# Another order of issue for the first image of a four-layer vision kernel, and weighing before copying in layer 1

## The chip, the cores and the metric

The kernel runs on one core of a Trainium2 chip. Its engines each work through their own queue in order: TensorE (PE, matmuls; PEld is its weight load), VectorE (DVE), ScalarE (ACT), GpSimd (POOL) and SyncE (SP, which here only issues DMAs). ACT and POOL issue DMAs too. The metric is the device time of one execution in microseconds, lower is better. All data are float32; one float32 matmul appears in the trace as two PE instructions.

## The reference

The input is a batch of four images of 32 x 32 pixels with 384 channels. Four residual layers follow one another, each on a group-normalized input (32 groups of 12 channels):

```
x = x + L0(gn(x))   # deformable attention, 6 heads of 64
x = x + L1(gn(x))   # attention weighted by a group similarity, 12 heads of 32
x = x + L2(gn(x))   # box-filtered energy ratio
x = x + L3(gn(x))   # 3 x 3 outlook attention
```

Layer 0, cut to what matters:

```
q = x @ w_q + b_q
o = gelu(layernorm(grouped 3x3 conv(q)))                 # 6 groups of 64 channels
offset = tanh(o @ w_offp) * 16 ; pos = offset + pixel    # per group and pixel
xs = bilinear_sample(x, pos)                             # a gather of 1024 positions in 6 groups
k = xs @ w_k + b_k ; v = xs @ w_v + b_v
bias = bilinear_sample(rpe, (pixel - pos) / 2)           # 1024 x 1024 per head
out = softmax(q k^T / 8 + bias) v @ w_out + b_out
```

Layer 1, the part that the change touches, per head:

```
sim = sigmoid(beta + alpha * cos(xg, gc))                # 1024 x 256
gw  = (sim sim^T) * gamma + (1 - gamma)                  # 1024 x 1024, symmetric
a   = softmax(q k^T / sqrt(32)) * gw
a   = a / (sum of a over the queries + 1e-8) ; out = a v
```

## The kernel before

An image's channels lie in 3 blocks of 128 partitions (KC), its 1024 pixels in 8 tiles of 128 (NJ). Two lanes of work are issued by Python generators. The *front* (class Front) computes layer 0 of one image; the *trunk* (class Trunk) computes layers 1 to 3 of the image before it. `Net.layer0` (L266) issues the whole of layer 0 of image 0 alone; from then on `Net.layer3` (L280) steps the trunk of image b and, after each step, as many steps of the fronts of images 1 to 3 as keep them level. Within this program a planner of the framework chooses each engine's order: an instruction may be moved ahead of its place in the program if its inputs and memory are free in the planner's model; `keep_in_program_order` (the name `pin`) forbids that for single instructions. The framework also puts a wait between two engines that use the same PSUM bank, in program order, and between users of the same SBUF memory.

SBUF scopes are stacked from two sides: the front's on the right, the trunk's on the left; a scope's tiles can be written once the tiles that lay there before are released. PSUM holds two tiles of two banks (`big`) and four of one bank (`bank`). Weights rotate through three buffers (`weights`, L242).

Image 0, in the order of the program:

- `consts` (L107) loads small constants: `rows` (a row of 874 KB once broadcast to 128 partitions, L128), `hall` (L138), `Wa` (L154) on SP, others on ACT; it computes `gam` by a sigmoid on ACT (L158) and `half` on DVE (L166).
- `normed` (L551) loads the image on SP (L557), transposes it on PE (L567), copies it on ACT (L572) and normalizes it by `norm_steps` (L329), a generator that yields between the two sums over groups (PE, L345) and what reads them. For image 0 it calls `windows` (L173), which interpolates the table of `rpe` to half steps (DVE, L185 to L192; `half`, L193) and cuts it into 6 x 16 overlapping strips by six DMAs in DRAM, issued on ACT (L198). Then it transposes the normalized image, and ACT copies it (L596, two buffers) for SP to write to `pairs` in DRAM (L598).
- `inputs0` (L610) computes queries into `qpad` (L625), the grouped convolution (L644), the layer norm, the gelu and the positions (DVE), then gathers (POOL, L714) tile by tile, weighs on DVE (L727 to L730), transposes on PE (L741). After the last tile come the keys (`w_k`, L770, through DRAM `k0`) and then the values (`w_v`, L776, L777).
- `heads0` (L866) is a pipeline of 96 blocks (6 heads, 2 halves of queries, 8 tiles of keys), turn by turn, with DVE full almost throughout. From turn 17 on it takes one step of `early0` (L604) per turn, which normalizes image 1 ahead of time and stores it in DRAM (`xh1`). Each pair of heads ends in a division (`divide`, L913) of its block of `qpad`.
- `outputs0` (L457) multiplies `qpad` by `w_out` (18 matmuls by `dense_t`, L385: three blocks, two halves, three terms), adds the residual and stores `x1`.
- `Trunk.start` (L1115) loads `x1`, `image` (L1122) normalizes it; the front of image 1 begins with a load of `xh1` (L616, one DMA on SP) and its queries.

Layer 1 works on pairs of heads (`pair`, L1411). Each of its 6 pairs has 8 turns j; a turn computes two halves h of exponentials (`e`, L1486) and, for each half and each head r, one bank of group weights. Since these are symmetric, tiles above the diagonal are copied from the bank to `keep` by ACT (L1516; tiles `gn` and `gf`) and later transposed in place of a product (L1503). DVE weighs the exponentials by the bank and sums them (L1517). The next pair's row maxima and sums (`sums_step`, L1342: PE L1351, DVE L1359, ACT L1360) are interleaved.

## Time and profile before

| what | us |
|---|---|
| median of three executions (4630.12 to 4641.2) | 4640.76 |
| the profiled execution | 4625.18 |
| its span, first to last instruction | 4623.3 |
| PE busy | 4160.8 |
| DVE busy | 3134.6 |
| ACT busy | 2282.3 |
| POOL busy | 969.4 |
| mean granted clock of PE, share of full speed | 0.946 |

A busy time is the sum over an engine's instructions; what is missing to the span is idle. The views used below: the table of stretches gives busy time between two points of time; the timeline gives instructions in order, each with its start, its duration and, in brackets, how long its engine was idle before it and whose result ended that; the table of waits sums these by pairs (engine, tile and line waiting, then the engine, tile and line waited for; us in total, times, longest); the chain is followed backwards from the last instruction, at each step to what released it. A name with q (ACTq, SPq) is the engine's sequencer issuing a DMA. L with a number is a line of the program.

### The profile page before, as it was taken

The numbers are of one execution on the slowest core, as the hardware profiler recorded it, in microseconds if no ns is written. First come the engines' busy times: TensorE is split into PE (matmuls) and PEld (weight loads), VectorE is DVE, ScalarE is ACT, GpSimd is POOL, SyncE is SP. The second block draws the span as 40 slices with busy tenths as digits, with TensorE's granted clock in tenths as the row PEclk, the third lists the DMA queues.
The fourth block names the chain that finished last, engine by engine and source line by source line (L and its number), as shares of the span: only waits on it lengthen the run. The fifth ranks groups of instructions, "written<-read, shape, count | busy, mean of one in ns | idle before, by whom it ended". The sixth has DMA issues, their size and how long they took to land.

```text
span 4623.3 us, 47195 instructions
## 1 busy us (share of the span) xinstructions
PE 4160.8 (90%) x15896; PEld 1796.5 (39%) x15896; DVE 3134.6 (68%) x5909; ACT 2282.3 (49%) x3631; POOL 969.4 (21%) x994
## 2 busy tenths in 40 slices
PE   5499789999999898999999989899999999999998
PEld 2233334333334453333333444343333335343444
DVE  3599555878777627677878744768787874565644
ACT  2166333666565314565666432456665641555532
POOL 0654213212112104311212110522121211000000
PEclk8799899999999988999999989899999998999988
DMA  6445234212212244311212133432121213310011
GB/s 126 135 141 143 84 100 134 79 52 69 58 51 63 85 118 148 103 44 51 81 52 78 38 100 121 141 102 63 46 67 40 74 38 122 102 34 24 23 37 41
DMA packets 232819, 370.99 MB, mean 80 GB/s; under 512 B 117732, under 2 KB 165697, under 8 KB 232577
## 3 DMA queue, kind: packets, MB, share of 16 engines
q1 hardware_dynamic: 171560, 201.49, 14.7%
q0 software_dynamic: 39936, 145.53, 10.3%
q10 hardware_dynamic: 21080, 20.96, 1.8%
q8 instruction: 126, 2.06, 0.2%
q14 instruction: 117, 0.95, 0.1%
HBM read 287.90 MB, written 80.27 MB: 80 GB/s over the span
## 4 chain that ended last, share of the span: by engine, by line
PE 37%; DVE 8%; ACT 6%; issue 4%; DMA 2%; POOL 1%; SPq 0%; ACTq 0%; POOLq 0%; DVEq 0%
PE bank L1508 8%; PE big L1478 4%; PE bank L855 3%; PE bank L820 3%; PE big L1351 3%; PE bank L409 2%; ACT big L1360 2%; PE bank L1503 2%; PE big L395 2%; PE bank L1450 2%; DVE nmax L1359 2%; DVE e L1517 2%; PE bank L1188 1%; PE big L1633 1%; PE bank L1801 1%
## 5 line engine op out<-in xcount | busy, mean ns | idle before, releaser
L1508 PE MATMUL bank<-whole,sg 128*128 128x512 f32 (+3 forms) x2304 | 852.8, 505 | 8.3 <-POOL sg L1461 6.9
L1517 DVE SCALAR_TENSOR_TENSOR e<-bank,gam,e 128x512 f32<-128x512 f32 x768 | 561.4, 748 | 435.8 <-ACT gf L1516 157.5
L1360 ACT ACTIVATE big<-big,nmax 128x1024 f32<-128x1024 f32 x384 | 418.6, 1090 | 355.4 <-DVE nmax L1359 354.6
L1486 ACT ACTIVATE e<-big 128x1024 f32<-128x1024 f32 x384 | 379.8, 1019 | 415.2 <-PE big L1478 409.9
L1508 PEld LDWEIGHTS bank<-whole,sg 128*128 128x128 f32 x2304 | 402.7, 197 | 370.2 <-issue 281.0
L1359 DVE TENSOR_REDUCE nmax<-big 128x1 f32<-128x1024 f32 x384 | 454.1, 1217 | 51.9 <-PE big L1351 50.9
L799 POOL DMA_INDIRECT win<-strips,widx x288 | 307.9, 1069 | 680.4 <-DVE z L812 403.7
L1461 POOL TENSOR_SCALAR sg<-whole,gam 128x512 f32<-128x512 f32 x192 | 149.3, 780 | 1436.5 <-PE bank L1508 1013.3
L1478 PE MATMUL big<-qa,ka 64*128 64x512 f32 x1536 | 426.3, 627 | 11.2 <-ACT big L1360 10.7
L1351 PE MATMUL big<-k,q 32*128 32x512 f32 x1536 | 320.7, 659 | 78.8 <-ACT big L1360 40.0
L820 PE MATMUL bank<-qpad,kz 128*128 128x512 f32 x576 | 282.1, 618 | 12.4 <-DVE e L1517 12.4
L714 POOL DMA_INDIRECT gat<-pairs,sidx x192 | 207.3, 1079 | 386.3 <-DVE ix_gt L500 224.1
L855 PE MATMUL bank<-lg,va 128*64 128x512 f32 x576 | 263.7, 601 | 15.0 <-ACT lg L853 14.9
L855 PE MATMUL bank<-lg,ones 128*64 128x512 f32 x576 | 263.0, 601 | 0.0
L817 DVE SCALAR_TENSOR_TENSOR lg<-z,bias_f,lg 128x512 f32<-128x512 f32 x288 | 220.0, 772 | 37.8 <-ACT lg L816 36.4
L1478 PEld LDWEIGHTS big<-qa,ka 64*128 64x128 f32 x1536 | 138.8, 187 | 270.4 <-issue 157.1
L811 ACT ACTIVATE z<-win,bias_f 128x528 f32<-128x528 f32 x288 | 207.9, 738 | 58.5 <-DVE lg L817 26.3
L812 DVE SCALAR_TENSOR_TENSOR z<-win,bias_f,z 128x528 f32<-128x528 f32 x288 | 213.9, 759 | 25.5 <-ACT z L811 23.5
L852 DVE TENSOR_TENSOR lg<-lg,tb 128x512 f32<-128x512 f32 x288 | 187.5, 696 | 42.4 <-ACT tb L845 42.4
L1450 PE MATMUL bank<-e,vs 128*32 128x512 f32 x1536 | 206.7, 604 | 0.9 <-DVE vs L1444 0.9
L821 DVE TENSOR_TENSOR lg<-bank,lg 128x512 f32<-128x512 f32 x288 | 191.5, 683 | 21.3 <-PE bank L820 20.2
L816 ACT ACTIVATE lg<-z,bias_f 128x512 f32<-128x512 f32 x288 | 200.3, 718 | 11.3 <-DVE z L812 5.1
(313 smaller groups left out, 6617.7 us busy)
## 6 DMA issues: line engine op xcount, KB each, us to landing
pairs<-xn SPq DMA_DIRECT2D x64, 192.0 KB
q<-qd SPq DMA_DIRECT2D x48, 256.0 KB
w<-in_gmat SPq DMA_DIRECT2D x16, 576.0 KB
w<-in_w_off SPq DMA_DIRECT2D x12, 576.0 KB
w<-in_Wqkv SPq DMA_DIRECT2D x12, 576.0 KB
a<-in_x SPq DMA_DIRECT2D x16, 384.0 KB
x<-a ACTq DMA_DIRECT2D x4, 1536.0 KB
win<-strips,widx POOLq DMA_INDIRECT x384, 3.9
```

The lines of the kernel that those rows point to most:

```text
L799: nc.gpsimd.indirect_dma_start(out=win, out_offset=None, in_=self.strips[:, :], in_offset=bass.IndirectOffsetOnAxis(ap=self.widx[:, q, c : ...
L817: v.scalar_tensor_tensor(lg, z[:, :, 1 : HW + 1], sc(0, 0), lg, ALU.mult, ALU.add)
L820: nc.tensor.matmul(ps, kz[:, j * P : (j + 1) * P], both, start=True, stop=True)
L855: nc.tensor.matmul(po[out, :], w, lf, start=j == 0, stop=j == NJ - 1)
L1351: nc.tensor.matmul(ps[r][:, h * 512 : (h + 1) * 512], self.q4[rows, i * P : (i + 1) * P], self.k4[rows, 0:512], start=True, stop=True,)
L1359: v.tensor_reduce(nmax[:, r, i : i + 1], ps[r], AX.X, ALU.max, negate=True)
L1360: nc.scalar.activation(ps[r], ps[r], AF.Exp, bias=nmax[:, r, i : i + 1], accum_out=den[:, r, i : i + 1],)
L1450: nc.tensor.matmul(av[r0 : r0 + HD1, :], vs[:, r, :], es[h][:, r, :], start=j == 0, stop=j == NJ - 1,)
L1478: nc.tensor.matmul(ps[:, r, :], ka[rows, j * P : (j + 1) * P], qa[rows, cols], start=True, stop=True,)
L1486: nc.scalar.activation(e, ps, AF.Exp)
L1508: nc.tensor.matmul(ps[:, (mid - i0) * P :], sg[:, r, m, :], sim[:, h, r, m, (mid - i0) * P :], start=m == 0, stop=m == 1,)
L1517: v.scalar_tensor_tensor(e[:, r, :], ps, self.gam[:, 1:2], e[:, r, :], ALU.add, ALU.mult, accum_out=tot[:, r, h : h + 1],)
```

## The change

Image 0 and the start of image 1:

- `rows`, `hall` and `Wa` are loaded in a new function `more_consts`, called after the image's loads; `gam` and `half` are computed at the end of `windows`.
- The six strips are issued by a new function `cut`, on SP, after the convolution.
- `norm_steps` yields three times instead of once after each of its two sums. Only `early0` takes these yields one at a time.
- In the gather loop the values of tile j - 2 follow the weighing of tile j; `w_v` is loaded before the loop, the keys follow it, and the last tile's values come after the keys.
- `outputs0` of image 0 first issues the terms 0 and 1 of blocks 0 and 1, then the rest. It runs inside the heads' scope, its tiles on the left.
- Image 1's `xh1` is loaded by three DMAs on ACT.

For all images: in `pair`, ACT's copy to `keep` is issued after DVE's weighing of the same bank. No arithmetic changes.

```diff
@@ -124,8 +124,6 @@
                 )
-        self.rows = self.ct([P, NROW], "rows")
-        nc.sync.dma_start(self.rows, a["rows"].partition_broadcast(P))
         self.blk = self.ct([P, P], "blk")
@@ -134,8 +132,6 @@
         nc.gpsimd.memset(self.hall, 0.0)
-        for k in range(KC):
-            nc.sync.dma_start(self.hall[32 * k : 32 * k + 4, :], a["blk"][0::32, :])
         self.sel = self.ct([81, 9, 25], "sel")
@@ -150,23 +146,16 @@
+    def more_consts(self):
+        nc, a = self.nc, self.a
+        self.rows = self.ct([P, NROW], "rows")
+        nc.sync.dma_start(self.rows, a["rows"].partition_broadcast(P))
+        for k in range(KC):
+            nc.sync.dma_start(self.hall[32 * k : 32 * k + 4, :], a["blk"][0::32, :])
         self.wa = self.ct([P, KC, 81], "Wa")
...
-        self.gam = self.ct([P, 2], "gam")
-        nc.scalar.activation(
-            self.gam[:, 0:1], self.rows[:, R_SCAL + 2 : R_SCAL + 3], AF.Sigmoid
-        )
-        nc.vector.tensor_scalar(
-            self.gam[:, 1:2], self.gam[:, 0:1], -1.0, 1.0, ALU.mult, ALU.add
-        )
-        self.half = self.ct([P, 2], "half")
-        nc.vector.tensor_scalar(
-            self.half, self.rows[:, R_SCAL : R_SCAL + 2], 0.5, None, ALU.mult
-        )
     def col(self, i, k):
@@ -174,7 +163,7 @@
         v = nc.vector
-        half = self.dram.tile([G, UP, UP], F32, tag="half", name="half")
+        self.steps = half = self.dram.tile([G, UP, UP], F32, tag="half", name="half")
         self.strips = self.dram.tile([G * NSTRIP * STRIP, 1], F32, tag="strips", name="strips")
@@ -191,11 +180,28 @@
                 nc.scalar.dma_start(half[:, i::2, :].rearrange("g r c -> r g c"), u[0:m])
+        self.gam = self.ct([P, 2], "gam")
+        nc.scalar.activation(
+            self.gam[:, 0:1], self.rows[:, R_SCAL + 2 : R_SCAL + 3], AF.Sigmoid
+        )
+        nc.vector.tensor_scalar(
+            self.gam[:, 1:2], self.gam[:, 0:1], -1.0, 1.0, ALU.mult, ALU.add
+        )
+        self.half = self.ct([P, 2], "half")
+        nc.vector.tensor_scalar(
+            self.half, self.rows[:, R_SCAL : R_SCAL + 2], 0.5, None, ALU.mult
+        )
+    def cut(self):
         dst = self.strips.rearrange("(g s r c) o -> g s r (c o)", g=G, s=NSTRIP, c=WROW)
         for g in range(G):
-            row = half[g]
+            row = self.steps[g]
             src = bass.AP(row.tensor, row.offset, [[4, NSTRIP], [UP, UP], [1, WROW]])
-            nc.scalar.dma_start(dst[g], src)
+            self.nc.sync.dma_start(dst[g], src)
@@ -353,7 +359,7 @@
         sums = groups(mv[:, :, 0:1])
-        yield
+        yield from (None,) * 3
         nc.vector.tensor_scalar(mean, sums, 1.0 / 12.0, None, ALU.mult)
@@ -364,7 +370,7 @@
         sums = groups(d)
-        yield
+        yield from (None,) * 3
         nc.scalar.activation(rstd, sums, AF.Sqrt, bias=self.eps[:, 0:1], scale=1.0 / 12.0)
@@ -382,12 +388,14 @@
-    def dense_t(self, w, src, ko, lo=0):
+    def dense_t(self, w, src, ko, lo=0, kis=range(KC), ps=None):
         nc = self.nc
-        ps = self.big()
+        if ps is None:
+            ps = self.big()
         for h in range(2):
-            for ki in range(KC):
+            for ki in kis:
                 if len(src.shape) == 4:
@@ -439,7 +447,9 @@
                     yield from self.heads
-                yield from self.outputs0(b)
+                    self.side = "left"
+                    yield from self.outputs0(b)
+                    self.side = "right"
                 return
@@ -458,12 +468,21 @@
             w = self.weights("w_out")
+            ps = {}
+            if b == 0:
+                for ko in range(2):
+                    ps[ko] = self.dense_t(w, self.qpad, ko, kis=(0, 1))
             for ko in range(KC):
...
                 nc.sync.dma_start(x, self.x0[b % 2][rows, :])
-                ps = self.dense_t(w, self.qpad, ko)
-                v.scalar_tensor_tensor(x, ps, self.col(C_BOUT, ko), x, ALU.add, ALU.add)
+                if ko in ps:
+                    ps[KC] = self.dense_t(w, self.qpad, ko, kis=(2,), ps=ps[ko])
+                else:
+                    ps[KC] = self.dense_t(w, self.qpad, ko)
+                v.scalar_tensor_tensor(x, ps[KC], self.col(C_BOUT, ko), x, ALU.add, ALU.add)
                 nc.sync.dma_start(self.x1[b % 2][rows, :], x)
@@ -555,6 +574,8 @@
             nc.sync.dma_start(xin[:, j : j + 2, :], src[:, j : j + 2, :])
+        if b == 0:
+            self.net.more_consts()
         x = self.wt([P, KC, N], "a12", 2)
@@ -613,7 +634,8 @@
             xh = self.wt([P, KC, N], "a12", 2)
-            nc.sync.dma_start(xh, self.xh1.rearrange("(k p) n -> p k n", p=P))
+            for k in range(KC):
+                nc.scalar.dma_start(xh[:, k], self.xh1[k * P : (k + 1) * P, :])
             yield 25
@@ -653,6 +675,8 @@
             yield 15
+        if b == 0:
+            self.cut()
         oall = self.wt([P, NJ, C], "a12", 2)
@@ -750,6 +774,13 @@
         gats, xss = {0: gather(0), 1: gather(1)}, {}
+        va, bv = self.va, self.rows[:, R_BV0 : R_BV0 + C]
+        if b == 0:
+            w = self.weights("w_v")
+        def value(j):
+            v.tensor_tensor(va[:, j, :], self.dense_n(xsT, w, j), bv, ALU.add)
         yield 8
@@ -758,23 +789,23 @@
                 xss[j] = weigh(j, gats.pop(j))
+            if b == 0 and j > 1:
+                value(j - 2)
             if j > 0:
...
             next(self.heads)
-        va = self.va
         kT = self.wt([P, KC, N], "a12", 2)
-        w = self.weights("w_k")
+        wk = self.weights("w_k")
         for ko in range(KC):
-            ps = self.dense_t(w, xsT, ko)
+            ps = self.dense_t(wk, xsT, ko)
             v.tensor_scalar(kT[:, ko, :], ps, self.col(C_BK, ko), GC**-0.5, ALU.add, ALU.mult)
             nc.sync.dma_start(self.k0[ko * P : (ko + 1) * P, :], kT[:, ko, :])
-        bv = self.rows[:, R_BV0 : R_BV0 + C]
-        w = self.weights("w_v")
-        for j in range(NJ):
-            ps = self.dense_n(xsT, w, j)
-            v.tensor_tensor(va[:, j, :], ps, bv, ALU.add)
+        if b > 0:
+            w = self.weights("w_v")
+        for j in range(NJ - 1 if b == 0 else 0, NJ):
+            value(j)
         yield 30
@@ -1512,12 +1543,12 @@
                             )
-                    if first < i1:
-                        nc.scalar.copy(keep[:, r, :], ps[:, (first - i0) * P :])
                     v.scalar_tensor_tensor(
...
                     )
+                    if first < i1:
+                        nc.scalar.copy(keep[:, r, :], ps[:, (first - i0) * P :])
                 if h == 0 and st:
```

## The prediction

> **What bounds the kernel now.** I read the totals first, then busy time by stage, then the order of instructions inside the stages where TensorE is not full.
>
> ```profile
> PE 4160.8 (90%) x15896; PEld 1796.5 (39%) x15896; DVE 3134.6 (68%) x5909; ACT 2282.3 (49%) x3631; POOL 969.4 (21%) x994
> ```
>
> TensorE is the bound, and all it can win back is its 462 us of idle time. The next table gives, for each stretch, the busy time of PE, PE weight load, DVE, ACT and POOL, then the granted clock, the DMA share and GB/s.
>
> ```profile
> 50.00:56.00 6.00, 1.78 (x11) 1.11 (x14) 0.00 (x0) 2.25 (x4) 0.00 (x0) 0.89 1.65 55
> 126.00:187.00 61.00, 14.74 (x38) 7.20 (x38) 23.22 (x21) 3.77 (x9) 45.96 (x43) 0.58 0.37 112
> 187.00:215.00 28.00, 28.00 (x74) 14.45 (x73) 10.19 (x14) 3.32 (x6) 2.84 (x3) 0.92 0.36 118
> 531.00:540.00 9.00, 0.73 (x3) 0.03 (x1) 0.95 (x2) 1.29 (x2) 0.00 (x0) 0.78 0.23 60
> 554.00:571.00 17.00, 6.19 (x27) 5.93 (x27) 6.13 (x14) 0.00 (x0) 4.62 (x3) 0.57 0.69 241
> 571.00:590.00 19.00, 19.00 (x42) 8.31 (x46) 2.44 (x4) 2.68 (x4) 0.00 (x0) 0.84 0.09 32
> 1950.00:2600.00 650.00, 606.85 (x2424) 243.87 (x2417) 514.78 (x1021) 400.58 (x644) 127.87 (x132) 0.97 0.20 59
> ```
>
> Image 0's layer 0 runs alone up to 531 us. While POOL gathers (126 to 187 us) TensorE stands idle 46 us; straight after, it is full for 28 us with nothing beside it. There are holes at 50, 531 and 554 us. In the long loops (last row) it is idle 43 us in 650. The timeline shows what lies at each place:
>
> ```profile
> 39.37 14.34 ACTq L198 DMA_DIRECT2D strips<-half  x6
> 53.75 0.86 ACT L596 COPY xn<-bank 128x384 f32<-128x384 f32 x2 [13.32 <-DMA strips<-half]
> 54.28 1.28 PE L590 MATMUL bank<-ident,a 128*128 128x128 f32 x6 [4.05 <-ACT xn L596]
> ...
> 199.72 15.00 PE L409 MATMUL bank<-w,a 128*128 128x384 f32 x46
> ```
>
> ACT spends 14.34 us issuing the strips; TensorE's transposes wait 4.05 us for the ACT copy behind them. At 199.72 the values' matmuls hold up the first logits (L984, 214.55).
>
> ```profile
> 539.97 13.71 PE L395 MATMUL big<-qpad,w 128*128 128x512 f32 x28 [8.27 <-DVE qpad L913]
> 557.36 0.59 PE L345 MATMUL bank<-gn_mv,w 128*128 128x1 f32 x2 [3.68 <-DVE gn_mv L316]
> ...
> 571.28 18.50 PE L395 MATMUL big<-a,w 128*128 128x512 f32 x36
> ```
>
> After image 0's last heads TensorE waits for the last division, computes outputs, waits through layer 1's normalization, and only then does image 1's queries (18.50 us). For layer 1, the waits by line and the chain that ended last (start, us, what):
>
> ```profile
> DVE e L1517 <- ACT gf L1516: 157.5, 101, 2.1
> DVE e L1517 <- ACT gn L1516: 157.2, 156, 4.0
> ```
>
> ```profile
> 2052.25 1.08 ACT big L1360
> 2053.34 0.04 issue
> 2053.38 1.21 ACT big L1360 x2
> 2054.59 0.48 ACT gf L1516
> 2055.07 0.03 issue
> 2055.10 1.44 DVE e L1517 x4
> ```
>
> The weighing on DVE sits behind a copy on ACT, which sits behind two exponentials.
>
> **The change part by part.** The profiled execution took 4625.2 us (span 4623.3 and 1.9 around it); the runs' median is 4640.8, 15.6 higher. I sum against 4625.2 and carry the gain to 4640.8.
>
> *Constants after the image.* The rows load (874 KB) leaves the head of SP's queue; three hall loads and Wa follow image 0's four loads too. The first image load now waits 3.3 us for the rows to land (SP's waits). But ACT also lost 2.9 us behind the first half-step DMA, whose data come from the table load on ACT's own queue, and that stays. Gain between 0 (that DMA alone sets the pace) and 6.2 (3.3 + 2.9); I take 4. gmat moves behind these loads: issued at 15.34 and first read at 22.3, it has 7 us of cover; without that cover TensorE waits for it. The sigmoid for gam moves behind windows and takes its 1.28 us table load along, into ACT's waits: cost 0 to 1.3, I take 1.
>
> *Strips from ACT to SP.* Six issues leave ACT (14.34 us). TensorE gets back the 4.05 us. On SP they stand behind the convolution, before w_k and w_v (issued at 72 us, first read after 126), hidden as long as strips land before the first window gather at 135.7; issue plus the observed 33 us of traffic from 72 ends near 105. Between 0 (SP issues them early, in front of the pairs writes, and ACT waits for those: 12.8 us of such waits exist) and 4.05; I take 4.
>
> By the Trainium skill's page "DMA: Bandwidth & Descriptors", section "Issuing engines are not separate DMA queues", moving an issue to another engine saves only the sequencer's time, which it calls usually small. By that rule this term would be near 0 and the total 4 less. The 14.34 us row here differs, and the row decides.
>
> *Values into the gather loop.* Of 48 value instructions (15.0 us for 46, 0.326 each) seven of eight tiles, 42, move into TensorE's 46 idle us. There they cost nothing on the path; DVE's seven additions (0.56 us each) fit as well, as DVE is busy only 23 of 61 us. If the gathers did not leave these holes, the same work would cost its 13.7 us again. What remains after the last gather is the keys' 12.25 us and the last tile. 42 x 0.326 = 13.7 less about 0.7 for the last key's trip through DRAM. Between 9 (the key tiles, reloaded at 196.5, land late) and 13.7; I take 13.
>
> *Two longer pauses in image 1's early normalization.* DVE waited 3.8 us for L345 at 320 us, in a stage where DVE is full. Four more turns of the heads' loop hide it. 0 to 3.8; I take 3.5.
>
> *Outputs begun before the last division.* The planner had already hoisted 8 of 36 instructions (36 minus the 28 above). The new code puts 16 there: 8 x 0.43 = 3.4 us into the 8.27 us hole. 0 to 3.4; I take 3. The outputs' tiles now lie on the left, beside the heads' tiles.
>
> *Image 1's queries.* Their input was loaded on SP at 560.66, after the outputs' tiles were released. With those on the left and three loads on ACT (three issues of about 0.4 us, the L616 row) it can arrive long before. Then TensorE can run 18.5 us of queries in the hole of 554 to 571, where it is idle 17 - 6.2 = 10.8 us at a clock of 0.57; warm, the queries need 36 x 0.43 = 15.5. The hole takes 10.8, the warm clock saves 3, and the outputs' earlier end lets some more in: I take 15, between 0 (the planner leaves them behind the normalization, or POOL's 2.99 us clearing of qpad comes late) and 18.5. Behind ACT's loads in its queue stand the heads' exponentials; should they reach the queue before their memory is free, ACT stands, as it did 13.32 us for the strips.
>
> *Weighing before copy.* 480 copies (288 of 372 ns, 192 of 577 ns median). The wait turns round: the copy now waits for DVE. The chain from 1962 us on carries 25.9 us of L1516 pieces; scaled from the 2050 us of layer 1's pairs in it to 3000 in all, 38 us is the most. The other end: in the 480 - 257 = 223 cases where DVE came late anyway, the copy (mean 0.454 us) had been hidden and now adds to the bank's time: 223 x 0.454 = 101 us lost. I take +8: TensorE's waits that name L1517 sum to only 20.6 us, the nearest row.
>
> The Trainium skill's page "PSUM — Partial Sum Buffer", section "PSUM bank collisions raise a hardware error", says that two engines must not access one bank on the same partitions together, reads included. The 257 waits between two readers agree. By that rule the swap moves the wait and removes none, which makes this term 0 and the total 8 less.
>
> Sum: 4 - 1 + 4 + 13 + 3.5 + 3 + 15 + 8 = 49.5. The profiled execution becomes 4575.7, the median 4640.8 - 49.5 = 4591.
>
> **The rivals.**
> (1) The gain at the seam is swallowed: at 671 to 691 us TensorE is already idle 13.8 us waiting for image 1's gathers, so queries 15 us earlier may only lengthen that hole. Against it: those gathers hang on the same queries and move with them. With the swap at 0 as well: 4591 + 15 + 8 = 4614.
> (2) The planner's order stays much as it was (it already loaded the outputs' residual at 372 us and started the keys in the gather loop): only strips, constants and half the values remain, 4 - 1 + 4 + 6.5 = 13.5, so 4627 or above, up to 4641: no change. Against it: it did not put one value tile into 46 idle us.
> (3) Slower: the swap's lower end. ACT is in order; a copy waiting for a late DVE holds the exponentials behind it, and TensorE already waits 40.0 and 38.7 us at L1351 for ACT. At full price 4591 + 8 + 101 = 4700. It decides from (41.5 + 14) / 223 = 0.25 us per late case. Against it: ACT is busy 62% in those loops, DVE 79%, and the chain shows DVE behind ACT.
>
> **How the numbers follow.** Forecast (4562 to 4610) 0.68; rival 1 0.15; rival 2 0.08; rival 3 0.09. About 0.3% (14 us) is what a measurement of this kernel can tell from no change: faster 0.83, same 0.08, slower 0.09. The likeliest gives 4591; the range 4562 to 4632 takes in rival 1 and part of 2; below lies the swap's upper end.
>
> **What would show it.** In the changed profile: strips issues on SP and no 4 us wait at L590; value matmuls between the gathers and L984 starting about 21 us earlier; L345 no longer holding DVE near 300; 20 instructions instead of 28 after the last division; queries before 571 less the shift; ACT's copy waiting for L1517, with TensorE's waits at L820 and L1503 smaller. The prediction is wrong if TensorE's waits for ACT at L1351 grow by tens of us, or if the shift present at 600 us is gone at 750.

## The result and the profile after

The changed kernel took 4583.9 us (median of six runs, 4576.8 to 4598.1), the kernel before 4641.6 us beside it: a ratio of 0.988, 95% interval 0.986 to 0.9899. The forecast was 4591. The profiled execution took 4579.9 us, its span 4578.1 us, which is 45.2 us less than the span before. The medians are 57.7 us apart: the profiled execution before (4625.18) was faster than all six of its timed runs (4630.1 to 4648.9), so the profiles show less than the runs.

Lines have other numbers now. Those used below: L321 statistics and L351 group sums of a normalization, L174 to L181 the half-step tables, L204 strips, L617 the copy of a transposed block, L403 dense matmuls, L647 queries into qpad, L666 convolution, L738 gathers, L417 values, L1015 logits of image 0's heads, L944 their division, L480, L485 and L486 the outputs' residual load, addition and store, L638 the load of image 1's normalized input, L830 to L886 a head of a later image, L1382, L1390 and L1391 matmul, row maximum and exponential of layer 1's sums, L1492 the first operation of a pair, L1509 and L1539 its matmuls, L1534 its transposes of kept copies, L1546 and L1551 the weighing and the copy, L1639 the first matmuls of layer 2.

The totals of the profile after:

```profile
PE 4150.6 (91%) x15896; PEld 1795.0 (39%) x15896; DVE 3138.6 (69%) x5909; ACT 2303.6 (50%) x3633; POOL 972.6 (21%) x994
```

TensorE's idle time fell from 462 to 427 us; its busy time fell too, by 10 us, with the same number of instructions. The table of stretches, each row where the same work lies now (columns as before the change):

```profile
44.00:50.00 6.00, 6.00 (x22) 2.51 (x24) 0.00 (x0) 1.31 (x2) 0.00 (x0) 1.00 0.00 0
122.00:183.00 61.00, 30.82 (x70) 16.25 (x71) 25.36 (x27) 2.88 (x6) 46.48 (x43) 0.70 0.37 112
183.00:200.00 17.00, 17.00 (x40) 8.14 (x39) 7.13 (x9) 3.73 (x6) 2.84 (x3) 0.88 0.52 151
513.00:522.00 9.00, 3.98 (x10) 1.44 (x8) 0.64 (x2) 0.68 (x2) 0.00 (x0) 0.98 0.19 53
536.00:553.00 17.00, 9.32 (x35) 6.07 (x36) 6.21 (x16) 1.55 (x2) 3.16 (x3) 0.68 0.60 219
553.00:567.00 14.00, 14.00 (x34) 5.91 (x36) 2.10 (x3) 2.24 (x2) 0.00 (x0) 0.90 0.13 43
1926.00:2576.00 650.00, 609.90 (x2447) 244.36 (x2446) 519.48 (x1025) 404.25 (x641) 127.44 (x131) 0.98 0.22 61
```

While POOL gathers (second row) TensorE is busy 31 us, it was 15; the full stretch behind it is 17 us in place of 28. The hole at the strips is closed (first row). The hole at the seam (fifth row) is not: TensorE is idle 7.7 us of 17, at a clock of 0.68, and 14 us of queries still follow. In layer 1 (last row) it is idle 40 us in 650 instead of 43. The timeline at the strips, the values and the seam:

```profile
36.65 0.64 SPq L204 DMA_DIRECT2D strips<-half  x1
...
63.84 10.35 SPq L204 DMA_DIRECT2D strips<-half  x5
...
182.86 4.05 PE L417 MATMUL bank<-w,a 128*128 128x384 f32 x6
...
197.18 2.10 PE L417 MATMUL bank<-w,a 128*128 128x384 f32 x6
...
199.12 1.02 PE L1015 MATMUL big<-qpad,kz 128*128 128x512 f32 x2
...
522.37 11.85 PE L403 MATMUL big<-qpad,w 128*128 128x512 f32 x20 [5.38 <-DVE qpad L944]
...
535.69 1.28 DVE L485 SCALAR_TENSOR_TENSOR res<-big,cols,res 128x1024 f32<-128x1024 f32 x1 [5.33 <-DMA res<-x]
...
540.10 1.32 ACTq L638 DMA_DIRECT2D a<-xh  x3
...
545.58 3.59 PE L403 MATMUL big<-a,w 128*128 128x512 f32 x4 [4.28 <-DMA a<-xh]
```

The strips have left ACT, and no transpose waits for them. Only the last value tile stands between the keys and the first logits, which start at 199.1 instead of 214.6. After the division TensorE has 20 output matmuls left instead of 28. But image 1's input is not there early: its load is issued at 540.10, after the third residual addition, which itself waited 5.33 us for its residual to land. For layer 1 the table of waits (us in total, times, longest) and the chain that ended last (start, us, what):

```profile
DVE e L1546 <- PE bank L1539: 226.7, 232, 3.8
...
ACT gn L1551 <- DVE e L1546: 134.1, 122, 4.1
DVE e L1546 <- PE bank L1534: 120.9, 51, 5.0
...
ACT gf L1551 <- DVE e L1546: 50.3, 80, 3.2
```

```profile
2033.85 1.43 DVE e L1546 x4
2035.28 1.21 DVE lg L883 x2
2036.49 2.27 DVE nmax L1390 x2
2038.75 0.67 DVE e L1546 x2
2039.42 1.46 DVE lg L883 x2
```

The 314.7 us in which VectorE waited for the copies are gone. It waits for TensorE now; its idle time before the weighings is 349 us in all, where it was 434. ScalarE waits 184 us for VectorE instead. Weighings stand in the chain one behind the other, without copies between them.

Where the 45.2 us came from, by the times at which the same work ends in the two traces (an estimate by subtraction, good to a few us only: in three executions of the changed kernel, image 1's gathers from first to last took 72, 78 and 79 us):

| step | forecast | in the traces |
|---|---|---|
| constants, up to the first group sums (22.3 to 21.5) | 4 | 0.8 |
| strips, up to the end of the convolution | 4 | 4.9 |
| sigmoid's table load, up to the first gather | -1 | -1.6 |
| gathers | 0 | -0.6 |
| values, up to the first logits | 13 | 12.0 |
| heads with the longer pauses | 3.5 | 2.1 |
| outputs | 3 | 1.9 |
| image 1's queries | 15 | 3.3 |
| from there to layer 1's first pair (739.1 to 717.5) | 0 | -1.2 |
| layer 1 of four images and all after | 8 | 23.6 |
| sum | 49.5 | 45.2 |

So the total was nearly met with two terms far off in opposite directions: the queries gave 12 us too little, the weighing 15 too much. The experiments are on these two first.

### The profile page after: what moved, and what is told of

Read it like the earlier page. It is cut to its first block, busy times and chain, and to the rows that moved or that the text cites. A ratio compares the mean times of both kernels' runs of the same rounds, so it can differ in the third digit from the quotient of the medians.

```text
span 4578.1 us, 47313 instructions
## 1 busy us (share of the span) xinstructions
PE 4150.6 (91%) x15896; PEld 1795.0 (39%) x15896; DVE 3138.6 (69%) x5909; ACT 2303.6 (50%) x3633; POOL 972.6 (21%) x994
## 4 chain that ended last, share of the span: by engine, by line
PE 56%; DVE 14%; ACT 7%; issue 5%; DMA 4%; POOL 2%; SPq 0%; ACTq 0%; DVEq 0%; POOLq 0%
PE bank L1539 13%; PE big L1509 5%; PE big L1382 4%; PE bank L851 4%; PE big L403 4%; PE bank L886 4%; PE bank L417 4%; PE bank L1534 3%; PE bank L1481 3%; DVE nmax L1390 2%; DVE e L1546 2%; PE bank L1219 2%; PE big L666 2%; PE big L1664 1%; POOL gat L738 1%
## 5 line engine op out<-in xcount | busy, mean ns | idle before, releaser
L1539 PE MATMUL bank<-whole,sg 128*128 128x512 f32 (+3 forms) x2304 | 852.5, 505 | 7.0 <-POOL sg L1492 7.0
L1546 DVE SCALAR_TENSOR_TENSOR e<-bank,gam,e 128x512 f32<-128x512 f32 x768 | 561.9, 747 | 349.2 <-PE bank L1539 226.7
L1391 ACT ACTIVATE big<-big,nmax 128x1024 f32<-128x1024 f32 x384 | 417.6, 1087 | 322.3 <-DVE nmax L1390 322.1
L1517 ACT ACTIVATE e<-big 128x1024 f32<-128x1024 f32 x384 | 379.7, 1019 | 363.2 <-PE big L1509 362.1
L1539 PEld LDWEIGHTS bank<-whole,sg 128*128 128x128 f32 x2304 | 403.4, 197 | 369.6 <-issue 281.6
L1390 DVE TENSOR_REDUCE nmax<-big 128x1 f32<-128x1024 f32 x384 | 454.5, 1219 | 76.4 <-PE big L1382 75.9
L830 POOL DMA_INDIRECT win<-strips,widx x288 | 316.2, 1098 | 658.0 <-DVE z L843 391.8
L1492 POOL TENSOR_SCALAR sg<-whole,gam 128x512 f32<-128x512 f32 x192 | 143.7, 750 | 1442.6 <-PE bank L1539 1019.6
L1509 PE MATMUL big<-qa,ka 64*128 64x512 f32 x1536 | 417.8, 630 | 9.7 <-ACT big L1391 9.5
L1382 PE MATMUL big<-k,q 32*128 32x512 f32 x1536 | 327.7, 674 | 82.2 <-ACT big L1391 45.2
L738 POOL DMA_INDIRECT gat<-pairs,sidx x192 | 209.2, 1090 | 378.8 <-DVE ix_gt L519 217.4
L886 PE MATMUL bank<-lg,va 128*64 128x512 f32 x576 | 265.6, 605 | 15.0 <-ACT lg L884 14.9
L886 PE MATMUL bank<-lg,ones 128*64 128x512 f32 x576 | 265.0, 605 | 0.0
L1509 PEld LDWEIGHTS big<-qa,ka 64*128 64x128 f32 x1536 | 135.7, 188 | 256.3 <-issue 124.3
L852 DVE TENSOR_TENSOR lg<-bank,lg 128x512 f32<-128x512 f32 x288 | 192.9, 685 | 49.4 <-PE bank L851 48.1
```

The lines of the kernel that those rows point to most:

```text
L738: nc.gpsimd.indirect_dma_start(out=gat[:, g].rearrange("p l c -> p (l c)"), out_offset=None, in_=pairs[:, :], in_offset=bass.IndirectOffse ...
L830: nc.gpsimd.indirect_dma_start(out=win, out_offset=None, in_=self.strips[:, :], in_offset=bass.IndirectOffsetOnAxis(ap=self.widx[:, q, c : ...
L886: nc.tensor.matmul(po[out, :], w, lf, start=j == 0, stop=j == NJ - 1)
L1382: nc.tensor.matmul(ps[r][:, h * 512 : (h + 1) * 512], self.q4[rows, i * P : (i + 1) * P], self.k4[rows, 0:512], start=True, stop=True,)
L1390: v.tensor_reduce(nmax[:, r, i : i + 1], ps[r], AX.X, ALU.max, negate=True)
L1391: nc.scalar.activation(ps[r], ps[r], AF.Exp, bias=nmax[:, r, i : i + 1], accum_out=den[:, r, i : i + 1],)
```

## The experiments

They ran on three other chips, on which the kernel before took 4662 to 4670 us; so ratios to it are given, and runs of one group shared chip and runs of the kernel before.

| run | median us | before beside it | ratio | 95% interval |
|---|---|---|---|---|
| e1_swap_alone | 4636.2 | 4670.5 | 0.9923 | 0.9902 to 0.9944 |
| e2_no_swap | 4640.1 | 4670.5 | 0.9939 | 0.9919 to 0.9958 |
| e3_residual_in_spent | 4604.0 | 4670.5 | 0.9859 | 0.9838 to 0.988 |
| e6_tables_pool | 4608.2 | 4670.5 | 0.9873 | 0.9848 to 0.9897 |
| c1_changed_again (the changed kernel, for its times beside the next three) | 4615.8 | 4662.3 | 0.9896 | 0.9881 to 0.9911 |
| e4_values_late | 4619.9 | 4662.3 | 0.991 | 0.9891 to 0.993 |
| e5_strips_act | 4624.9 | 4662.3 | 0.993 | 0.9911 to 0.995 |
| e7_swap_narrow_only | 4620.8 | 4662.3 | 0.9917 | 0.9902 to 0.9931 |
| c2_changed_again (the same, beside the next three) | 4610.8 | 4666.7 | 0.9882 | 0.9861 to 0.9902 |
| e8_residual_and_tables | 4587.7 | 4666.7 | 0.983 | 0.9809 to 0.9852 |
| e9_seam_undone | 4616.1 | 4666.7 | 0.9895 | 0.9874 to 0.9916 |
| e10_front_as_before | 4623.2 | 4666.7 | 0.9914 | 0.9893 to 0.9936 |

c1 and c2 are the changed kernel itself:

> The changed kernel as it is, so that the others of this call have its times and its profile from the same chip. All theories: about 0.988 of before.

> The changed kernel as it is, for its times and profile beside the three others on one chip. All theories: about 0.989 of before.

### The exchange alone, without it, and half of it

e1 is the kernel before with only this edit; e2 is the changed kernel with it undone:

```diff
-                    if first < i1:
-                        nc.scalar.copy(keep[:, r, :], ps[:, (first - i0) * P :])
                     v.scalar_tensor_tensor(
                         e[:, r, :], ps, self.gam[:, 1:2], e[:, r, :], ALU.add, ALU.mult,
                         accum_out=tot[:, r, h : h + 1],
                     )
+                    if first < i1:
+                        nc.scalar.copy(keep[:, r, :], ps[:, (first - i0) * P :])
```

> The kernel before with the weighing of L1517 put ahead of the copy of L1516, nothing else. Theory A (the exchange itself is worth what layer 1's loops gained, 45.2 of the span less 21.6 up to image 0's first pair = 23.6 us): about 20 to 24 us faster than before, 4618 us (0.995 to 0.996), with the gain growing pair by pair in every image and nothing before 739 us. Theory B (the exchange is worth the 8 us of the prediction, or nothing, and the rest of the 23.6 us came from the lanes standing differently against each other after the earlier start of image 0): 4632 us or more (0.998 to 1.000).

> The changed kernel with the copy ahead of the weighing again, as before. Theory A: 20 to 24 us are lost against the changed kernel, 4606 us (0.992 to 0.993 of before), and the gain over the kernel before stays at about 21 us from image 0's first pair to the end. Theory B: 4592 us or less (0.988 to 0.990), the gain still grows through the images.

e7 turns only the narrow copies round; the wide ones precede the weighing:

```diff
+                    if first < i1 and h != j // 4:
+                        nc.scalar.copy(keep[:, r, :], ps[:, (first - i0) * P :])
                     v.scalar_tensor_tensor(
...
-                    if first < i1:
+                    if first < i1 and h == j // 4:
                         nc.scalar.copy(keep[:, r, :], ps[:, (first - i0) * P :])
```

> The changed kernel with the weighing first only where the copy is of the pair's own half (gn, 288 copies, 1 to 3 blocks); the 192 copies of whole tiles (gf, 577 ns) stand ahead of the weighing, as before the change. Theory L (the gain goes by the waits of VectorE that are removed, 157.5 us behind gf and 157.2 behind gn): half of the 25 to 30 us of the exchange is lost, 12 to 15 us above the changed kernel, ratio 0.991. Theory M (only the whole tiles' copies count: they are needed last, two or more blocks later, and hold the weighing longest, so turning them is all profit, while a narrow copy is needed by the next block's transposes): nearly all is lost, 22 us or more, ratio 0.993. Theory N (the narrow ones make it): 4 us or less is lost.

By whole times the exchange is worth 36 us on the kernel before (1 - 0.9923 of 4670; interval 26 to 46; 34 by the medians), and taking it from the changed kernel costs some 20 to 27 us (0.9939 against 0.9882 to 0.9896 of the unchanged kernel on other chips). A cleaner reading is the length of the four stages from an image's first pair (L1492) to layer 2's first matmul (L1639), summed over the images; an earlier start does not enter it:

| kernel | sum of the four stages, us |
|---|---|
| copy first: before; e2 | 2850.2; 2862.4 |
| narrow copies turned: e7 | 2846.6 |
| weighing first: e10; e9; e6; after; c1; c2 | 2822.2; 2825.6; 2827.2; 2827.8; 2830.4; 2830.7 |
| weighing first, continued: e5; e8; e3; e1; e4 | 2833.5; 2834.2; 2835.0; 2837.5; 2841.5 |

On one chip that is 24.9 us (e2 to e1), 27.4 (e2 to e3) or 35.2 (e2 to e6), and 22.4 between the two kernels. But the eleven traces with weighing first differ by 19 us among themselves, mostly with the granted clock: their stages of images 0 to 2 last 776.0 to 778.8 us at a clock of 0.976, and 786.0 at the lowest, 0.961 (c2, image 2). With the clock taken out (an estimate, by a straight line in the granted clock through the 56 stages of the fourteen traces), copying first makes a stage 6.4 us longer in images 0 to 2 and 8.2 in image 3, 27 us in sum. Theory A is right in kind, and its 20 to 24 us are somewhat low; theory B falls. Half the exchange loses 16.2 us against c1 on the same chip, 13.1 and 5.1 against e5 and e4 there, and 16 with the clock taken out (4.4 us a stage, 2.5 in image 3), near the 12 to 15 of theory L: M and N fall by these lengths; the whole time says less (0.9917 against 0.9896, with overlapping intervals).

Where does it sit? The table of stretches for the four stages, first without the exchange (e2), then with it (e6, the changed kernel but for a part at the front). The first row is image 0's; the second is a stage in which both had a clock of 0.976, image 2's in e2 and image 1's in e6; the sum is over all four:

```profile
723.40:1509.90 786.50, 734.64 (x2842) 298.71 (x2839) 602.11 (x1168) 458.19 (x736) 156.60 (x159) 0.97 0.22 64
...
2983.10:3766.40 783.30, 729.96 (x2841) 296.18 (x2838) 600.68 (x1168) 458.09 (x736) 156.74 (x159) 0.98 0.22 64
...
sum 2862.40, PE 2680.84 PEld 1103.47 DVE 2097.89 ACT 1643.42 POOL 503.00; mean PE 670.21 PEld 275.87 DVE 524.47 ACT 410.86 POOL 125.75
```

```profile
716.70:1493.80 777.10, 726.00 (x2842) 295.81 (x2839) 603.23 (x1168) 463.62 (x736) 156.07 (x159) 0.98 0.23 65
1842.40:2618.60 776.20, 726.25 (x2841) 295.56 (x2838) 603.53 (x1168) 463.84 (x736) 155.86 (x159) 0.98 0.23 65
...
sum 2827.20, PE 2655.30 PEld 1096.80 DVE 2102.07 ACT 1662.51 POOL 502.94; mean PE 663.82 PEld 274.20 DVE 525.52 ACT 415.63 POOL 125.73
```

TensorE's idle time in them falls from 181.6 to 171.9 us, only 9.7 us. The other 25.5 us are time that the profile books as busy, for the same matmuls. Part of that is the clock, which was higher in e6. But busy time falls at an equal clock too, from 729.96 to 726.25 us in the second rows; by the same straight lines it is 4.0 us in a stage of images 0 to 2 and 5.7 in image 3, some 18 of the 27 us, and idle time is the rest. What becomes shorter inside the busy time is not shown; a stay in the pipeline behind a bank that is not free would fit.

### Image 1's queries

In the program, the first load of L638 waits for the third residual addition (L485) and for the three stores of x1 to land: its memory lies over the residual tiles of the outputs, on the left side as well. e3 takes those tiles away; image 0's last head has no more use for its keys and values:

```diff
-                x = self.wt([P, N], "res", 2)
+                if b == 0:
+                    va = self.va.rearrange("p j c -> p (j c)")
+                    x = (self.kz[0], self.kz[1], va[:, 0:N])[ko]
+                else:
+                    x = self.wt([P, N], "res", 2)
```

> The changed kernel, but image 0's three residual tiles of the outputs lie in the two key tiles and the value tile, which the last head has used up, in place of two tiles of their own (L479). Image 1's load of its normalized input then waits for no tile of the outputs, and the third residual for no buffer. Theory C (that load, issued at 540 us only after the last x1 store, and the third residual's wait of 5.33 us are what kept the queries' term at 3.3 of the 15 us of the prediction): the first query matmul right after the outputs' last, about 532 in place of 545 us, and 8 to 14 us of span less: 4570 to 4576 us (0.985 to 0.986). Theory D (the gain at the seam is swallowed by the wait for image 1's gathers, where TensorE stands idle at 650 to 670 us): queries earlier, but the first pair of layer 1 at most 3 us earlier, 4581 to 4584 us.

The timeline of e3 (its lines are 4 higher from L480 on), first ScalarE's queue, then TensorE and VectorE:

```profile
368.10 0.35 ACTq L642 DMA_DIRECT2D a<-xh  x1
...
374.24 0.33 ACTq L642 DMA_DIRECT2D a<-xh  x1
...
521.28 10.46 PE L403 MATMUL big<-qpad,w 128*128 128x512 f32 x20 [5.74 <-DVE qpad L948]
...
531.58 3.59 PE L403 MATMUL big<-a,w 128*128 128x512 f32 x8
531.78 1.28 DVE L489 SCALAR_TENSOR_TENSOR va<-big,cols,va 128x1024 f32<-128x1024 f32 x1 [3.88 <-PE big L403]
```

The input is loaded at 368 us instead of 540, queries follow the outputs without a gap, and the third addition waits only for its matmul. Image 1's convolution starts at 551.2 (566.9 after the change). The first pair of layer 1 comes at 710.1, 13.3 us before that of e2 on the same chip (e2 is the changed kernel up to there), where theory D allowed 3. So theory C holds for the places. For the whole time e3 alone is unclear: 0.9859 is theory C's figure, but its interval reaches to theory D's.

e9 goes the other way: outputs on the right, all after the division, one load on SP.

```diff
-                    self.side = "left"
-                    yield from self.outputs0(b)
-                    self.side = "right"
+                yield from self.outputs0(b)
...
-            if b == 0:
+            if False:
                 for ko in range(2):
                     ps[ko] = self.dense_t(w, self.qpad, ko, kis=(0, 1))
...
-            for k in range(KC):
-                nc.scalar.dma_start(xh[:, k], self.xh1[k * P : (k + 1) * P, :])
+            nc.sync.dma_start(xh, self.xh1.rearrange("(k p) n -> p k n", p=P))
```

> The changed kernel with the seam as before: the outputs' tiles on the right, all their matmuls after the last division, image 1's input in one load on SP. Theory (from the milestones of the change: outputs 1.9, queries 3.3 us): image 1's queries end 5 us later than in the changed kernel and the whole is 4 to 5 us longer, ratio 0.990. Rival (the seam is worth the 18 us of the prediction, and some other part of the change hides it): 15 us longer, 0.992.

Image 1's queries end at 573.9 instead of 569.8 (c2), and the whole is 5 us longer by the medians, which the intervals do not separate. That fits the 5.2 us of the two steps in the table; 15 us it is not.

### The front: constants, tables, strips

After the change VectorE does the half-step tables ahead of the statistics. Its timeline, changed kernel and then e6, in which GpSimd does them:

```profile
17.03 0.46 DVE L174 TENSOR_TENSOR t<-t,t 48x294 f32<-48x294 f32 x1 [1.46 <-DMA t<-in_rpe]
...
18.80 2.46 DVE L321 BATCH_NORM_STATS2 gn_st<-a 128x6 f32<-128x512 f32 x4
```

```profile
15.03 2.47 DVE L321 BATCH_NORM_STATS2 gn_st<-a 128x6 f32<-128x512 f32 x4
...
15.86 0.80 POOL L174 TENSOR_TENSOR t<-t,t 48x294 f32<-48x294 f32 x1 [0.19 <-DMA t<-in_rpe]
```

The edit is `nc.gpsimd` for `nc.vector` in windows, for L174 to L181.

> The changed kernel with the half-step tables' additions, copies and scalings (L174 to L181) on GpSimd in place of VectorE. Theory E (VectorE's table work, behind a load that lands at 17.0 us, stands ahead of the first statistics and holds them from 15.2 to 18.8 us; that is the 3.2 us missing from the constants' 4): the first statistics start at about 15.3, image 0's queries end 3 to 3.6 us earlier and the whole is 3 us shorter. Theory F (another wait ends there next, the group matrix or the sqrt table): the statistics start earlier but the queries end less than 1 us earlier, and the time stays.

Statistics start at 15.03 and the queries of image 0 end at 46.2, where the changed kernel's end at 48.6 to 49.4 in three executions: 2.4 to 3.2 us, by theory E. (With the five other runs that have the same front, the range is 47.9 to 50.3, so 1.7 to 4.1 us.) The whole time cannot show so little.

The last copy of the image ends at 15.2 us. So the constants' move did bring the image in early, and the second table's load, which lands at 17.0 us and whose addition stands ahead of the statistics in VectorE's order, took nearly all of it back.

e5 puts the strips' issues back on ScalarE, directly after windows; e10 puts back the whole front (constants, windows, sigmoid and strips as before).

```diff
-            self.nc.sync.dma_start(dst[g], src)
+            self.nc.scalar.dma_start(dst[g], src)
...
             self.windows()
+            self.cut()
...
-        if b == 0:
-            self.cut()
```

> The changed kernel with the six strips issued on ScalarE inside the windows again. Theory I (the issues hold the copies of TensorE's transposes; 4 us): the first convolution 4 to 6 us later, the whole 4 to 5 us longer, ratio 0.989. Theory K (a rule for moved issues: only the queue's own time is saved, nothing waits for it): the convolution starts less than 1 us later and the time stays.

> The changed kernel with the constants, the windows, the sigmoid and the strips' issues as before, all that follows the front as changed. With the strips alone back on ScalarE the convolution started at 71.6 us, 16 us later than in the kernel before. Theory Q (the price of the strips on ScalarE depends on what stands behind them in its queue: with the image's work earlier, all of the transposes' copies stand behind them): here the convolution starts at 55 to 57 us, as before, 6 to 7 us later than in the changed kernel, and the whole is 5 to 7 us longer, ratio 0.990. Theory R (the 22 us are the strips' own and came from elsewhere in the change): it starts at 65 us or later, ratio 0.993.

The timeline of e5 (L612, L618 and L648 here are L611, L617 and L647 of the changed kernel):

```profile
36.80 19.40 ACTq L204 DMA_DIRECT2D strips<-half  x6
...
56.24 0.86 ACT L618 COPY xn<-bank 128x384 f32<-128x384 f32 x2 [20.52 <-DMA strips<-half]
...
56.78 1.54 PE L612 MATMUL bank<-ident,a 128*128 128x128 f32 x6 [13.12 <-ACT xn L618]
56.99 2.14 ACT L648 ACTIVATE qpad<-big,cols 128x1024 f32<-128x1024 f32 x2
```

Here all six issues stand ahead of seven of the eight copies and of all three queries' evictions, and the convolution starts at 71.6 us, 22.7 later than in c1. Both theories on it were too low: layer 2 of image 0 comes 19.9 us later, that of image 3 still 8.2, and the median is 9.0 us higher. In e10 the convolution starts at 61.1, between the bounds of theories Q and R: the order in ScalarE's queue is again that of the kernel before, but the six issues take 18.68 us, not 14.34, or the 15.55 of e1, which has that front too (its convolution starts at 57.6). Beside them SP issues two residual loads of the outputs (at 37.90), which lay at 372 and 376 us in the kernel before and can go early since the outputs' tiles lie on the left. That these loads lengthen the strips' issue was not tried by itself. The whole is 12.4 us longer than c2 by the medians (ratios 0.9914 and 0.9882, the intervals overlap a little).

### The values

e4 puts image 0's values, and the load of their weights, after the keys again.

```diff
-            if b == 0 and j > 1:
-                value(j - 2)
...
-        for j in range(NJ - 1 if b == 0 else 0, NJ):
+        for j in range(NJ):
```

> The changed kernel with image 0's values after its keys again, w_v's load with them. Theory G (the values fill the waits for the gathers and cost nothing there; worth 12 to 13 us): image 0's first logits 12 to 13 us later than in the changed kernel, the span the same amount longer, ratio to before 0.9905 to 0.991. Theory H (what is gained up to the first logits is swallowed further on, at the waits for image 1's gathers): the first logits later, the first pair of layer 1 less than 5 us later, 0.9885 to 0.989.

First logits at 207.6; in the other kernels with this front they lie at 196.0 to 201.6, so 6 to 12 us. Layer 1's first pair is 11.1 us later than in c1, layer 2 of images 0 to 2 10.9, 13.3 and 16.3, of image 3 6.9, and the median is 4 us higher, which the intervals do not separate. H falls, since the delay is whole at the first pair; G's 12 is at the upper edge. Part of it goes in image 3, where c1's profiled stage (498.3 us) was some 4 us longer than in after (494.6) and e4 (494.1), at a granted clock of 0.978 against 0.985 in both.

### A version that beats both

e8 is the changed kernel with the edits of e3 and e6.

> The two cures that did something in the profiles together: image 0's three residuals in the spent key and value tiles, and the half-step tables on GpSimd. Theory: both places are on the path, so image 0's queries end 2.5 us earlier, image 1's first query follows the outputs at once, the convolution of image 1 starts about 18 us earlier than in the changed kernel, and 7 to 11 us less in the end, ratio 0.987. Rival: the wait for image 1's gathers takes the seam's part back and 3 us are left, 0.989.

4587.7 us against 4610.8 for the changed kernel on the same chip: 23 us less, and 0.983 (0.9809 to 0.9852) of the kernel before, against 0.9882 (0.9861 to 0.9902). The first logits come 2.4 us earlier than in c2, image 1's convolution 19.1 (550.6 against 569.7), layer 1's first pair 25.0 (702.4 against 727.4, of which 6 are c2's longer gathers). The two profiled executions are only 12.5 us apart at their ends; e8's was the slowest of its five. The table of stretches at the seam, e8 first, then c2:

```profile
520.00:540.00 20.00, 19.29 (x46) 8.48 (x45) 7.27 (x10) 0.00 (x0) 11.84 (x19) 0.87 0.51 168
540.00:560.00 20.00, 20.00 (x128) 8.95 (x130) 4.58 (x11) 6.17 (x7) 3.03 (x3) 1.00 0.26 81
```

```profile
520.00:540.00 20.00, 12.19 (x22) 5.25 (x22) 8.02 (x11) 0.00 (x0) 14.88 (x21) 0.78 0.54 180
540.00:560.00 20.00, 15.85 (x40) 9.92 (x41) 4.58 (x11) 1.55 (x2) 0.00 (x0) 0.54 0.44 158
```

TensorE is full where it was idle 12 us, and the clock is 0.87 and 1.00 instead of 0.78 and 0.54. Both theories had too little for the medians, 7 to 11 and 3 us: the wait for image 1's gathers did not take the gain back.

## Why the prediction was right, and where it was not

**Queries, 15 taken, 3.3 found: the step that failed is "With those on the left and three loads on ACT it can arrive long before."** It could not: the left side moved the outputs' tiles, but image 1's input still lay over them, and so waited for their last store. I had read the move of a tile as its freedom without asking what stands in the memory of the waiting one. With that overlap gone the term has its forecast size: 16 us at the convolution in e8 (19.1 less 2.9 that its front brings). Even the 3.3 are not safe: from the end of the outputs to the end of the queries it took 36.1 us before, 32.6 to 32.8 in five traces with the changed seam and 36.0 to 37.4 in four, with a granted clock of 0.78 from 540 to 568 us in one of the five (after) and 0.67 in one of the four (c2).

**Weighing before copy, 8 taken, 23.6 in the traces of the change, 25 to 35 on one chip, 27 at an equal clock.** The mechanism (the chain through the copy) was right, the term was mis-sized. I chose "TensorE's waits that name L1517", 20.6 us, as the nearest row. Rows of idle time could not show it: TensorE's idle time in these stages fell by 9.7 us, about the 8 of the forecast, and at an equal clock its busy time by some 18. The premise "all it can win back is its 462 us of idle time" was wrong here. The scaled chain, 38 us, taken as the upper end, was the nearer row. The lower end, 101 us lost through hidden copies, did not occur: ScalarE waits 184 us for VectorE in 202 cases, and the waits that rival 3 hung on (L1351, now L1382, for ScalarE) went from 40.0 to 45.2 and from 38.7 to 36.8.

The prediction set against this term the Trainium skill's page "PSUM — Partial Sum Buffer", section "PSUM bank collisions raise a hardware error", by which two engines must not access one bank on the same partitions together, reads included. The traces agree that the two readers go in turn (314.7 us of waits one way, 184.4 the other). That the exchange is then worth nothing does not follow: some 27 us of the four stages depend on who goes first, and the chain after the change has weighings, not copies, one behind the other.

**Constants, 4 taken, 0.8 found**, inside its bounds. The forecast named the half-step DMA on ScalarE as what might set the pace; it was the table work on VectorE behind the same loads (e6 gives back 1.7 to 4.1).

**Strips, 4 taken, 4.9 found**, a little over the upper bound of 4.05. Right between the two kernels, but no property of the strips: with the constants moved, the same six issues on ScalarE cost 22.7 us at the convolution (e5), with the old front in the new kernel 12.5 (61.1 less c2's 48.6), of which 4.3 (18.68 less 14.34; 3.1 by e1's 15.55) are the longer issue. The terms of the sum are not independent. The Trainium skill's page "DMA: Bandwidth & Descriptors", section "Issuing engines are not separate DMA queues", says that issuing from several engines saves only the sequencer's time for starting a DMA, usually small relative to the DMA itself. That the term would be near 0, as the prediction read it, does not follow: here the sequencer's 19.40 us held a TensorE transpose for 13.12, and the measurement decides.

**Values, 13 taken, 12.0 found, 6 to 12 when undone.** Right in kind: the work lies in the gathers' waits. Of the 42 instructions that were to go there, six came at 182.86, where TensorE is full again; 36 x 0.326 is 11.7. **Pauses 2.1 for 3.5, outputs 1.9 for 3, table load -1.6 for -1:** right in kind by the times of the two traces (VectorE's wait of 3.80 us for the group sums of image 1 is 0 after the change); no run undid one of the three alone.

**Rivals.** Rival 1 (the seam's gain ends in the wait for gathers): the gathers moved with the queries, as the argument against it said; the lead of 22.8 us at the end of the queries is still 21.6 at the first pair. Rival 2 (the planner keeps its order): 42 value instructions did move. Rival 3: see above. So the forecast time was met by a right mechanism in most terms and by two errors of opposite sign, 12 too much and 15 too little. That these two nearly cancel is luck.

## What to carry to other kernels

A load moved to another queue or another side is early only if every tile that lies in its memory is dead by then; look for the last reader of that memory, not of the data. Where two engines read one PSUM tile in turn, let the one go first whose result is needed at once, and judge it by the length of the whole stage at an equal granted clock, since a stall can sit in what the profile books as busy. Terms that share a queue are not to be added as if they were independent: what an issue costs is what stands behind it, and an earlier start changes that.

## What the runs showed of the chip

Six issues of the same strips took 14.34 us on ScalarE's queue in the kernel before and 15.55 in e1, 18.68 and 19.40 us where two residual loads went out beside them, and on SP 0.64 us for the first and 10.35 for the other five.

TensorE's booked busy time over some 2830 us of layer 1, with the same matmuls, depends on the order of two readers of its banks: some 18 us at an equal granted clock. It depends on the clock as well: 7 us in a stage of 780 for 0.01 of the granted clock (737.4 at 0.961, 723.0 at 0.980, both with weighing first).

The gathers of image 1 took 72, 78 and 79 us from first to last in three executions of one program on three chips, and 71 and 80 in the kernel before and e1, which do the same up to there; so one profile does not settle a difference of less than 8 us in that stage.
